# Splitting and joining DMA-turned attention probabilities at later places in an interleaved kernel

## The chip, the cores and the metric

The kernel runs on one core of a Trainium2 chip. The metric is the device time of one execution in microseconds (us), given as the median of several runs; lower is better. A profile of one execution stands beside it.

## The reference

The input is 128 graphs of 64 nodes with 768 features in float32, and a boolean adjacency per graph. Two layers follow one another, both with a residual and a layer norm:

```python
# layer 0: 12 heads of 64, additive attention, gated
h = einsum('bnd,ade->bane', x, W); th = tanh(h)
attn = leaky(th @ w_src + swap(th @ w_dst)); attn = where(adj, attn, -999); attn = softmax(attn)
feat = elu(attn @ h + b);  gate = sigmoid(x @ H_w.T + H_b)
x = layernorm(x + gate * feat + (1 - gate) * x)
# layer 1: 6 heads of 128, dot-product attention under the same adjacency
q, k, v = (heads(x @ Wi + bi) for Wi, bi in ((Wq, bq), (Wk, bk), (Wv, bv)))
probs = softmax(q @ k.T / sqrt(128) + where(adj, 0, -9e15))
x = layernorm(x + (probs @ v) @ Wf + bf)
```

The change touches layer 1's attention alone.

## The kernel before

All arithmetic is float32. The 8192 rows are 64 tiles of 128 rows (two graphs each). Every large matrix product is a block product of seven products instead of eight (a `Job`); one such product is three 128-deep slices, six matmul instructions in the profile.

**The first stage** (until about 1530 us) does layer 0 for all tiles, projects the values of layer 1, and leaves the layer's rows (`x1_d`), their transposes (`x1T_d`) and the values (`v_d`) in DRAM. The change isn't in it.

**The second stage** works on 16 groups `g` of four tiles (eight graphs). Group 0 has its queries and keys begun in the first stage. From group 1 on a group is four stretches of 14 products each: three **feature pairs** (`fc` = 0, 1, 2), each of a query job and a key job for heads `fc` and `fc + 3`, and one **output pair**, which multiplies the contexts of the group before by `Wf`. I call them the first, second and third feature pair and the output pair. The order of the 14 products in a pair is `WOVEN`: q1 k1 q2 k2 q6 k6 q5 q7 k5 k7 q4 q3 k4 k3. Products 1, 6, 7 and 4 of a job add up in one PSUM bank `y`, 5 and 3 in a bank `z`, 2 stands alone in a bank `x`. So q6 may start only when ACT has copied q1's result out of `y` (L346), q7 only after q6's copy, q4 after q7's; the same for k. The results of `x` and `z` are added by DVE (L347).

The order of instructions on each engine's queue is written by hand. `step(job, i)` issues the product and then `flush()`, the way out of the product **before** it. `woven` then resumes the side generators once each, in a fixed order:

```python
        for k, i in order:
            step(pair[k], i)
            for s in sides:
                next(s, None)
```

The sides are, in this order: `older` (the attention begun in the last pair), `done` (the last layer norm and the stores, in a first feature pair), `rows` (`residuals`, in a third feature pair: it loads the residual rows `y` (L496), has POOL add the bias to them (L503), and DVE form the block sums for the output pair (L195 to L198)), and `attend` (the attention begun now). An attention's `yield`s therefore say beside which product of which pair each of its parts is issued. It is resumed 14 times as `attend` in its own pair, then 14 times as `older` in the next. Counting these resumptions, the attention whose probabilities are turned by DMA does:

| part | engine, line | resumption before |
|---|---|---|
| scores `sp` | PE L374 | 3 |
| mask and maximum `sc`, `mx` | DVE L383, L391 | 4 |
| subtract the maximum, exponential | DVE L393, ACT L394 | 5 |
| sum, reciprocal, normalize | DVE L398, L400, L401 | 7 |
| split: copy low and high 16-bit halves apart (two copies) | ACT L416 | 8 |
| write the halves to DRAM (`halvesd`) | SP L419 | 9 |
| two transposing DMAs back into `sc` | SP L427 | 12 |
| join: weave the halves together into `scT` (two copies) | ACT L434 | 15 (step 1 of the next pair) |
| probabilities times values `cp` | PE L460 | 20 (step 6 of the next pair) |
| bias and copy to `ctxT` (four) | ACT L473 | 21 (step 7 of the next pair) |

After a pair, the next attention is created and resumed once, which puts eight loads of its values `v` (L362) on SP's queue. Then SP's queue holds what comes next in program order: the residual rows of L496 at step 1 of a third feature pair, or the four loads `a` of the next group (L307) ahead of an output pair. SP issues in order: a DMA that waits holds back those behind it.

The very last attention (group 15, `fc` = 2) turns its probabilities on PE instead. In the last output pair it is resumed twice a step, and is followed by that group's own `residuals`, whose sums read the contexts of all heads.

Of the kernel before, what the change touches and what calls it, by code (L numbers as in the profile page):

```python
# [91 lines left out]
def kernel(  # L92
# [35 lines left out]
    def bank(tag, name, bufs=2):  # L128
        return ps.tile([P, 512], F32, tag=tag, name=name, bufs=bufs)
# [47 lines left out]
    def all_of(steps):  # L177
        for s in steps:
            s()
# [80 lines left out]
    def step(job, i):  # L260
        job.product(i)
        flush()
        behind.append((job, i))
# [19 lines left out]
    def load_adj(pool, t0, n, name):  # L283
        a = pool.tile([P, n, N], U8, tag="adj", name=name, bufs=2)
        nc.sync.dma_start(
            out=a, in_=adj[t0 * P : (t0 + n) * P, :].rearrange("(t p) m -> p t m", p=P)
        )
        return a
# [64 lines left out]
    def attention(g, fc, bias, by_dma=True):  # L353

        sb = pools["late"]
        qT, kT = qk.pop((g, fc))

        v = sb.tile([P, GT, 2, E1], F32, tag="v1", name=f"v1_{g}_{fc}")
        for a in range(2):
            c0 = (a * J1 + fc) * E1  # L360
            for i in range(GT):
                nc.sync.dma_start(  # L362
                    out=v[a * N : (a + 1) * N, i, :, :],
                    in_=v_d[GT * g + i][:, c0 : c0 + E1].rearrange("(g m) e -> m g e", m=N),
                )
        yield
        yield
        yield
        sp = bank("m", f"sp_{g}_{fc}")
        for i in range(GT):  # L370
            for a in range(2):
                for gr in range(2):
                    at = slice(i * P + gr * N, i * P + (gr + 1) * N)
                    T.matmul(  # L374
                        sp[gr * N : (gr + 1) * N, (i * 2 + a) * N : (i * 2 + a + 1) * N],
                        qT[:, a, at],
                        kT[:, a, at],
                        start=True,
                        stop=True,
                    )  # L380
        yield
        sc = sb.tile([P, GT, 2, N], F32, tag="sc", name=f"sc_{g}_{fc}")
        V.tensor_tensor(  # L383
            sc,
            sp.rearrange("p (i a m) -> p i a m", i=GT, a=2),
            bias.unsqueeze(2).to_broadcast([P, GT, 2, N]),
            ALU.add,
        )
        sc3 = sc.rearrange("p i a m -> p (i a) m")
        mx = small.tile([P, 2 * GT], F32, tag="mx1", name=f"mx1_{g}_{fc}")  # L390
        V.tensor_reduce(mx, sc3, AX.X, ALU.max)  # L391
        yield
        V.tensor_tensor(sc3, sc3, mx.unsqueeze(2).to_broadcast([P, 2 * GT, N]), ALU.subtract)  # L393
        S.activation(sc, sc, AF.Exp, scale=SCALE)  # L394
        yield
        yield
        den = small.tile([P, 2 * GT], F32, tag="den1", name=f"den1_{g}_{fc}")
        V.tensor_reduce(den, sc3, AX.X, ALU.add)  # L398
        rden = small.tile([P, 2 * GT], F32, tag="rden1", name=f"rden1_{g}_{fc}")
        V.reciprocal(rden, den)  # L400
        V.tensor_tensor(sc3, sc3, rden.unsqueeze(2).to_broadcast([P, 2 * GT, N]), ALU.mult)  # L401
        scT = sb.tile([P, GT * P], F32, tag="scT", name=f"scT_{g}_{fc}")
        if by_dma:


            yield
            apart, turned = (
                t.bitcast(U16).rearrange("p (h e) -> p h e", h=2)
                for t in (scT, sc.rearrange("p i a m -> p (i a m)"))
            )  # L410
            words, wordsT = (
                t.bitcast(U16).rearrange("p (e h) -> p h e", h=2)
                for t in (sc.rearrange("p i a m -> p (i a m)"), scT)
            )
            for h in range(2):
                S.copy(apart[:, h], words[:, h])  # L416
            yield
            dr = halves_d[(g * HK + fc) % 2]
            nc.sync.dma_start(  # L419
                out=dr.rearrange("h i p c -> p h i c"),  # L420
                in_=apart.rearrange("p h (i c) -> p h i c", c=P),
            )
            yield
            yield
            yield
            for h in range(2):
                nc.sync.dma_start_transpose(  # L427
                    out=turned[:, h], in_=dr[h].rearrange("i p c -> (i p) c")
                )
            yield  # L430
            yield
            yield
            for h in range(2):
                S.copy(wordsT[:, h], turned[:, h])  # L434
            yield
            yield
            yield
            yield
            yield
        else:  # L440
            yield
            yield
            sT = bank("m", f"sT_{g}_{fc}")
            for i in range(GT):
                T.transpose(
                    sT[:, i * P : (i + 1) * P], sc[:, i].rearrange("p a m -> p (a m)"), ident
                )
            yield
            S.copy(scT, sT)
            yield  # L450
            yield
        cp = [bank("m", f"cp_{g}_{fc}_{a}") for a in range(2)]
        for i in range(GT):
            for gr in range(2):
                at = slice(i * P + gr * N, i * P + (gr + 1) * N)
                for a in range(2):
                    rows = slice(a * N, (a + 1) * N)
                    for half in range(2):
                        e = slice(half * N, (half + 1) * N)
                        T.matmul(  # L460
                            cp[a][e, at], v[rows, i, gr, e], scT[rows, at], start=True, stop=True
                        )
        yield
        if g not in ctxT:
            ctxT[g] = [
                sb.tile([P, KC, W2], F32, tag="ctxT", name=f"ctxT_{g}_{pr}", bufs=4)
                for pr in range(2)
            ]

        for a in range(2):  # L470
            hd = a * J1 + fc
            for pr in range(2):
                S.activation(  # L473
                    ctxT[g][pr][:, hd, :],
                    cp[a][:, pr * W2 : (pr + 1) * W2],
                    AF.Identity,
                    bias=bias_c["v"][:, hd : hd + 1],
                )
# [80 lines left out]
    def woven(pair, *sides, order=WOVEN):  # L559
# [5 lines that stand above are left out]
# [467 lines left out]
    with ExitStack() as ph:  # L1032
# [24 lines left out]
        attend, older, done = attention(0, 0, biases[0]), nothing, nothing  # L1057
        next(attend)
        for g in range(NG):
            last = g == NG - 1  # L1060
            rows = residuals(g - 1, False) if g > 0 else last_weight()
            for fc in range(HK):
                if (g, fc) == (0, 0):
                    continue
                if fc == 1 and not last:
                    adjs[g + 1] = load_adj(sb, GT * (g + 1), GT, f"adjg_{g + 1}")
                if fc == 2 and not last:
                    biases[g + 1] = mask_bias(g + 1)
                if (g, fc) == (0, 1):
                    pair, order = (jobs["Q"], jobs["K"]), LAST_REST  # L1070
                else:
                    query_tiles(g, fc)
                    pair, order = feature_jobs(g, fc), WOVEN
                sides = [older] + [done] * (fc == 0) + [rows] * (fc == 2)
                woven(pair, *sides, attend, order=order)
                drain(*sides)
                older, attend = attend, attention(g, fc, biases[g], not (last and fc == 2))
                next(attend)
            if not last:
                sums = load_group(g + 1, G if g else (V, G))  # L1080
                if g:
                    all_of(sums)
                else:
                    done = in_turn(sums)
            if g > 0:
                pair = out_job(2 * g - 2), out_job(2 * g - 1)
                if last:
                    attend = chain(attend, residuals(g, True))
                woven(pair, older, *[attend] * (1 + last))
                drain(older)  # L1090
                if last:
                    drain(attend)
                older, attend = attend, nothing
                done = finish(2 * g - 2, 2 * g - 1)
        p = 2 * NG - 2
        pair = out_job(p), out_job(p + 1)
# [55 lines left out]
```

## Time and profile before

| | before |
|---|---|
| median of 3 runs | 3005.59 us (3001.39 to 3006.67) |
| profiled execution, its own time | 3001.74 us |
| its span, first to last instruction | 2999.9 us |
| PE busy | 2915.2 us (97%) |
| DVE, ACT, POOL busy | 1886.1, 1095.7, 830.3 us |
| mean granted TensorE clock | 0.992 |
| second stage | about 1530 to 3000 us |

PE is TensorE, DVE VectorE, ACT ScalarE, POOL GpSimd, SP the engine that issues all DMAs here; "PEld" are PE's weight loads. A row of the timeline gives start, duration, engine, line, operation, output<-inputs, shape, and in brackets how long the engine was idle before it and who ended the wait. Neighbouring rows of PE overlap a little, since matmuls are pipelined and their ends are modelled. A row of the table of stretches gives a stretch of time, its length, each engine's busy time with the number of instructions, the granted TensorE clock, the DMA engines' share and their GB/s.

### The profile page before, as it was taken

The page shows a single profiled execution, that of the slowest core. Times are in us where ns is not written, and L with a number is a line of the kernel's source. Part 1 is how long each engine was busy: PE and PEld are TensorE (multiplying, and loading weights), DVE is VectorE, ACT ScalarE, POOL GpSimd, SP SyncE. Part 2 cuts the span into 40 slices and gives each one's busy share as a digit, 9 for nine tenths or more (in the row PEclk, how much of TensorE's full clock was granted, in tenths as well). Part 3 has the DMA queues.
Part 4 walks back from the last instruction along what each step waited for, and adds up shares of the span by engine and source line. Part 5 has one row for each costly group of instructions (what it writes and reads, how often), then busy time and mean ns, then how long its engine had stood idle before and what let it go on. Part 6 is the DMA issues. An engine that isn't in the chain of part 4 may idle for free.

```text
span 2999.9 us, 45190 instructions
## 1 busy us (share of the span) xinstructions
PE 2915.2 (97%) x17860; PEld 2007.5 (67%) x17860; DVE 1886.1 (63%) x3019; ACT 1095.7 (37%) x1902; POOL 830.3 (28%) x648
## 2 busy tenths in 40 slices
PE   7999999999999999999899999999999999999998
PEld 4566666666666666666577777777777777777775
DVE  6878878888888788788834444444344444444445
ACT  2444444444444444444433333233322332332332
POOL 2333324324333333333401212211122211122121
PEclk9999999999999999999999999999999999999999
DMA  5333333333333334333433222232222323223322
GB/s 171 127 101 117 118 111 115 106 120 112 109 120 117 104 115 128 101 117 117 153 119 80 84 78 94 84 99 74 81 94 78 103 78 97 71 89 96 98 72 78
DMA packets 279700, 309.47 MB, mean 103 GB/s; under 512 B 146753, under 2 KB 213313, under 8 KB 279489
## 3 DMA queue, kind: packets, MB, share of 16 engines
q1 hardware_dynamic: 279488, 306.58, 32.2%
q8 instruction: 142, 2.33, 0.3%
q14 instruction: 70, 0.57, 0.1%
HBM read 167.81 MB, written 113.38 MB: 94 GB/s over the span
## 4 chain that ended last, share of the span: by engine, by line
PE 88%; DVE 8%; ACT 2%; DMA 1%; SPq 1%; issue 0%; POOL 0%; POOLq 0%; DVEq 0%; ACTq 0%
PE y_o L225 8%; PE y_v L225 8%; PE y_h L225 8%; PE y_g L225 8%; PE y_q L225 7%; PE y_k L225 7%; PE z_o L225 4%; PE z_v L225 4%; PE z_h L225 4%; PE z_g L225 4%; PE z_q L225 4%; PE z_k L225 3%; PE x_k L225 2%; PE x_o L225 2%; PE x_q L225 2%; PE x_h L225 2%
## 5 line engine op out<-in xcount | busy, mean ns | idle before, releaser
L503 POOL TENSOR_TENSOR y<-y,bf_bc 128x768 f32<-128x768 f32 x64 | 130.6, 2071 | 546.0 <-DMA y<-x1d 504.1
L841 POOL TENSOR_TENSOR x<-gate,x 128x768 f32<-128x768 f32 x64 | 117.4, 1835 | 323.8 <-ACT gate L892 309.0
L527 DVE TENSOR_TENSOR y<-y_o,y 128x384 f32<-128x384 f32 x128 | 71.3, 557 | 181.5 <-PE y_o L225 156.4
L225 PE MATMUL y_q<-a,w_wq 128*128 128x256 f32 x576 | 146.1, 391 | 32.4 <-ACT qT L346 32.4
L714 POOL TENSOR_TENSOR th<-th,wsd 128x768 f32<-128x768 f32 x64 | 117.3, 1833 | 182.4 <-DVE th L713 182.4
L225 PE MATMUL y_q<-sq_q,w_wq 128*128 128x256 f32 x576 | 142.2, 383 | 10.3 <-DVE sq_q L196 8.3
L394 ACT ACTIVATE sc<-sc 128x512 f32<-128x512 f32 x48 | 30.2, 630 | 325.4 <-DVE sc L393 325.4
L225 PEld LDWEIGHTS y_q<-a,w_wq 128*128 128x128 f32 x576 | 110.3, 194 | 56.9 <-ACT qT L346 38.8
L347 DVE TENSOR_TENSOR kT<-z_k,kT 128x256 f32<-128x256 f32 x96 | 40.7, 423 | 171.3 <-PE z_k L225 99.1
L225 PE MATMUL z_q<-sq_q,w_wq 128*128 128x256 f32 x576 | 145.9, 390 | 0.0
L225 PE MATMUL y_h<-w_wq,xT 128*128 128x384 f32 x384 | 136.2, 491 | 8.6 <-DMA w_wq<-in_w_dram 7.9
L347 DVE TENSOR_TENSOR qT<-z_q,qT 128x256 f32<-128x256 f32 x96 | 40.8, 425 | 164.6 <-ACT qT L346 101.1
L225 PE MATMUL y_k<-sq_q,hw_wk 128*128 128x256 f32 x576 | 141.1, 381 | 1.4 <-ACT kT L346 1.4
L225 PE MATMUL y_k<-a,hw_wk 128*128 128x256 f32 x576 | 141.3, 382 | 0.0
L225 PE MATMUL y_h<-w_wq,sx_x 128*128 128x384 f32 x384 | 136.5, 492 | 4.2 <-ACT h L674 4.2
L225 PE MATMUL z_k<-sq_q,hw_wk 128*128 128x256 f32 x576 | 140.0, 379 | 0.0
L225 PE MATMUL y_v<-wv,sv_v 128*128 128x384 f32 x384 | 136.6, 492 | 3.0 <-DVE sv_v L196 3.0
L225 PE MATMUL z_v<-wv,sv_v 128*128 128x384 f32 x384 | 137.5, 494 | 1.7 <-DVE v L704 1.7
L225 PE MATMUL z_h<-w_wq,sx_x 128*128 128x384 f32 x384 | 137.6, 495 | 0.5 <-DVE w_wq L171 0.5
L225 PE MATMUL y_g<-hw_wk,sx_x 128*128 128x384 f32 x384 | 135.0, 488 | 2.5 <-DVE hw_wk L174 2.2
L225 PE MATMUL y_v<-wv,x1T 128*128 128x384 f32 x384 | 136.1, 491 | 1.2 <-ACT x1T L791 1.0
L713 DVE TENSOR_TENSOR th<-th,wsd 128x768 f32<-128x768 f32 x64 | 67.6, 1056 | 108.7 <-ACT th L712 108.7
(175 smaller groups left out, 6730.8 us busy)
## 6 DMA issues: line engine op xcount, KB each, us to landing
x<-in_x_dram SPq DMA_DIRECT2D x64, 384.0 KB, 3.6
dd<-dstd SPq DMA_DIRECT2D x128, 192.0 KB, 3.4
x1d<-x SPq DMA_DIRECT2D x64, 384.0 KB, 2.6
x1Td<-x1T SPq DMA_DIRECT2D x32, 768.0 KB, 4.8
vd<-v SPq DMA_DIRECT2D x64, 384.0 KB, 2.9
a<-x1Td SPq DMA_DIRECT2D x64, 384.0 KB, 4.7
v<-vd SPq DMA_DIRECT2D x384, 64.0 KB, 2.3
y<-x1d SPq DMA_DIRECT2D x64, 384.0 KB, 4.4
```

The costliest lines, as they stand in the source:

```text
L225: T.matmul(to[:, : self.n], lhsT, rhs, start=kc == 0 and not more, stop=kc == HK - 1, skip_group_check=more,)
L347: lambda mn, bk_: V.tensor_tensor(at(*mn), bk_, at(*mn), ALU.add),
L394: S.activation(sc, sc, AF.Exp, scale=SCALE)
L503: G.tensor_tensor(y, y, pools["bf"], ALU.add)
L527: V.tensor_tensor(at(*mn), b, at(*mn), ALU.add)
L713: V.tensor_tensor(th[:, 0, :], th[:, 1, :], wsd[:, 0, :], ALU.mult)
L714: G.tensor_tensor(th[:, 1, :], th[:, 1, :], wsd[:, 1, :], ALU.mult)
L841: G.tensor_tensor(xp, st[t]["gate"], xp, ALU.mult)
```

## The change

Every part from the split on moves to a later resumption; no instruction is added or removed.

| part | before | after |
|---|---|---|
| split | 8 | 9 |
| write to DRAM | 9 | 10 |
| transposes | 12 | 13 |
| join | 15 (step 1) | 19 (step 5) |
| `cp` | 20 (step 6) | 22 (step 8) |
| `ctxT` | 21 (step 7) | 23 (step 9) |

In the last output pair `older` is now resumed twice a step too, so that the join is at its step 3, `cp` at step 4 and `ctxT` at step 5.

```diff
@@ attention, by_dma @@
             yield
+            yield
             apart, turned = (
...
                 nc.sync.dma_start_transpose(
                     out=turned[:, h], in_=dr[h].rearrange("i p c -> (i p) c")
                 )
-            yield
-            yield
-            yield
+            for _ in range(6):
+                yield
             for h in range(2):
                 S.copy(wordsT[:, h], turned[:, h])
-            yield
-            yield
             yield
             yield
             yield
@@ output pair @@
-                woven(pair, older, *[attend] * (1 + last))
+                woven(pair, *[older, attend] * (1 + last))
```

## The prediction

> **What bounds the kernel.** I read the busy line first, then who PE waits for in the second stage, then a table of its stretches, then one third feature pair in the timeline.
>
> ```profile
> PE 2915.2 (97%) x17860; PEld 2007.5 (67%) x17860; DVE 1886.1 (63%) x3019; ACT 1095.7 (37%) x1902; POOL 830.3 (28%) x648
> ```
>
> PE is the bound. From group 1 on, PE waits longer than 0.1 us for one thing only. The waits of PE and of ACT between 1590 and 2940 us (total us, times, longest):
>
> ```profile
> PE y_q L225 <- ACT qT L346: 33.3, 20, 2.2
> ...
> ACT scT L434 <- DMA sc<-halvesd: 88.6, 45, 5.5
> ...
> ACT scT L416 <- DVE sc L401: 58.4, 39, 3.0
> ```
>
> The join's wait for its DMA (88.6 us) is the larger one, and looks like the target; but PE's 20 waits are for `qT`, and the stretches say where they lie. I cut the stage at the first product of each pair. First comes group 1's second feature pair (1596.78), which has what a third one has on PE, 14 products, one `sp` and one `cp`, but no residual work beside it; then two of the 15 third feature pairs; then the sum over those 15:
>
> ```profile
> 1596.78:1617.47 20.69, 20.69 (x181) 17.83 (x180) 6.31 (x13) 8.31 (x19) 0.00 (x0) 1.00 0.22 55
> ...
> 1802.37:1827.07 24.70, 22.66 (x182) 18.93 (x181) 15.01 (x20) 7.87 (x19) 8.21 (x4) 0.93 0.34 104
> ...
> 1987.85:2011.42 23.57, 21.23 (x182) 17.67 (x180) 15.58 (x20) 7.73 (x18) 8.21 (x4) 1.00 0.34 106
> ...
> sum 356.16, PE 322.84 PEld 270.34 DVE 229.56 ACT 115.47 POOL 123.05; mean PE 21.52 PEld 18.02 DVE 15.30 ACT 7.70 POOL 8.20
> ```
>
> The 20.69 us of the first are all PE. So 15 x 20.7 = 310.5 us is the floor of the third pairs, and 356.2 - 310.5 = **45.7 us** is lost in them. All other feature and output pairs are gapless: 19.42, 19.41 and 29.66 us, equal in every group. Of the 45.7, 33.3 are the waits; in 4 of the 15 pairs the clock then falls to half for 3.4 us (the 0.93 above), 4 x 1.7 = 6.8 us; the remaining 5.6 go with the gaps' edges.
>
> The cause, in the pair from 1987.85:
>
> ```profile
> 1994.30 8.21 POOL L503 TENSOR_TENSOR y<-y,bf_bc 128x768 f32<-128x768 f32 x4 [35.06 <-DMA y<-x1d]
> ...
> 1994.92 1.60 DVE L196 TENSOR_TENSOR so_o<-so_o,ctxT 128x384 f32<-128x384 f32 x1
> ...
> 1996.45 2.30 DVE L393 TENSOR_TENSOR sc<-sc,mx 128x512 f32<-128x512 f32 x1
> ...
> 1999.83 1.56 PE L225 MATMUL y_q<-sq_q,w_wq 128*128 128x256 f32 x6 [0.18 <-ACT qT L346]
> ...
> 2003.79 0.69 DVE L401 TENSOR_TENSOR sc<-sc,rden 128x512 f32<-128x512 f32 x1
> ...
> 2004.57 1.14 ACT L416 COPY scT<-sc 128x512 uint16<-128x512 uint16 x2 [2.98 <-DVE sc L401]
> 2005.62 0.47 ACT L346 ACTIVATE qT<-y_q,bq_c 128x256 f32<-128x256 f32 x1
> ...
> 2006.13 1.56 PE L225 MATMUL y_q<-a,w_wq 128*128 128x256 f32 x6 [2.16 <-ACT qT L346]
> ```
>
> DVE reaches the normalization only at 2003.79, because each two-input operation beside POOL's four adds takes about 2.2 us (L393 takes 0.68 elsewhere). ACT stands at the split from about 2001.6. Behind the split is q7's copy, whose operands have long been there, and q4 needs it: PE loses 2.16 us. So the split, not the join, stops PE.
>
> **What the Trainium skill says.** GPSIMD Engine Reference, section 8 "Key points": GpSimd shares its SBUF interfaces with VectorE and contends with VectorE instructions that have two SBUF inputs. The trace agrees: L393 at 0.68 us without POOL, 2.30 with it. TensorE: Matmul & The Clock Gate, section "Architectural detail": ACT and DVE are strict FIFO. The trace agrees: q7's copy starts as the split ends. The same page, "Part 1: The HAM clock gate": half clock after idle, judged in a free-running window of 3413 ns. The trace shows four stretches of 3.4 us at 0.5, each right after one of these waits, and none in the other 11 groups.
>
> **The change, part by part.**
>
> *Split 8 to 9.* At step 9 the way out of q7 is issued first, so q7's copy is now ahead of the split. q4 is freed. Behind the split is now k7's copy (step 11), which k4 (step 13) needs, two products later than q4.
>
> *The write and transposes go with it, and so does SP's queue.* In the second feature pair:
>
> ```profile
> 1978.63 1.14 ACT L416 COPY scT<-sc 128x512 uint16<-128x512 uint16 x2 [0.46 <-DVE sc L401]
> ...
> 1980.28 0.47 ACT L346 ACTIVATE qT<-y_q,bq_c 128x256 f32<-128x256 f32 x1 [0.52 <-PE y_q L225]
> ```
>
> The split now follows q7's copy, 1980.65 to 1981.79 instead of 1978.63 to 1979.77: 2.0 us later. SP then goes without a pause:
>
> ```profile
> 1979.79 0.40 SPq L419 DMA_DIRECT2D halvesd<-scT  x1
> 1982.43 2.44 SPq L427 DMA_TRANSPOSE sc<-halvesd  x2
> 1984.97 5.67 SPq L362 DMA_DIRECT2D v<-vd  x8
> 1990.68 2.01 SPq L496 DMA_DIRECT2D y<-x1d  x4
> ```
>
> so the residual rows come 2.0 us later and POOL's adds start at 1996.3 instead of 1994.30. Counted from the pair's start, the 15 groups have POOL's start at 5.8 to 6.8 now and 7.8 to 8.8 after. L196 (from 7.07, 0.55 us) and L393 (7.55 to 8.24) then run ahead of POOL, and the exponential, q6's and k6's copies end near 9.3 and 9.7, 2 us earlier than now (11.9 and 12.3). That matters because of the next part.
>
> *cp from step 6 to 8.* Today its 1.1 us of PE lies between k6 and q7 and hides most of ACT's delay (only 0.18 us shows). After, q7 comes at 10.34 (two products of 1.29 from 7.75). It needs q6's copy: with 9.3 there is 1 us to spare; with today's 11.9 PE would wait 1.6.
>
> *Rest of the pair.* With POOL at P = 7.8 to 8.1 (9 groups), L197, L198 and the normalization each lose one 2.05-us add: normalization ends at P + 6.35 = 14.5 at worst. `ctxT`, now behind q7's copy, runs from cp's end 12.9 to 14.5 (four, 1.57 together). Split to 15.7, k7's copy 16.2; k4 at 18.1: free. DVE's add of q7 comes behind one more blocked sum, P + 8.8 = 16.6 to 16.9; q3 at 16.8 needs it: 0 to 0.2 us, I take 0.1 for nine groups, 1 us.
>
> *Join, step 1 to 5.* Two copies of 0.76 us. In a third pair they meet ACT idle from 3.3 to 8.3, and their data lands near 0.4. In a first pair ACT is idle for 3.18 us ahead of the layer norm (2044.3 to 2047.5): 1.53 fits. In an output pair ACT has nothing else. Nothing. If that cover were gone, 1.53 us in one pair per group, 23 us. The join's 88.6 us of waiting vanishes for no gain of its own.
>
> *First pair.* `ctxT` and two norms now precede k7's copy, which ends near 2056.6; k4 is at 2057.8. Nothing, with 1.2 us to spare. *Output pair:* the write is about 3 us later; the loads `a` were issued ahead, and their POOL sums have some 16 us to spare. *Group 0 to 1:* one 8.3-us wait for `a` behind slow transposes stays; 0 to 2 us worse, I take 0.5.
>
> *Last output pair.* cp two steps earlier than the PE-turned one's frees its PSUM banks: the waits of 0.93 and 0.40 us at 2947 to 2949 go, -1.3.
>
> Sum: -45.7 + 1.0 + 0.5 - 1.3 = **-45.5 us**. On the profile's own time, 3001.74 (span 2999.9 and 1.8 around it), 2956; it lay 3.9 below the median of the runs, so from the median **2960**.
>
> **Rivals.**
>
> *The wait moves to q7 (24%).* If POOL's adds don't start later (the rows are held by something else than the queue), q7 starts at 11.98 as now, and the pair is 11.98 + 7 x 1.295 + 1.1 + 0.3 = 22.4 us. Gain 356.2 - 15 x 22.4 = 20, and with the last pair's waits time 2985. For it: q6's copy is already late in five groups. Against: SP's queue shows no pause to take up the 2 us. Delays in between give values in between.
>
> *No difference (4%).* The copies freed are used up elsewhere, 3006.
>
> *Slower (11%): the join holds ACT.* At step 5 it stands ahead of the exponential and of q6's copy in all three feature pairs and cannot be passed. In a third pair its data is due at 0.4. From its start to the end of q6's copy are 1.53 + 0.63 + 0.47 = 2.6 us, so q7 (10.34) suffers when it comes after 7.7; q7 to the pair's end is 10.5, today's mean pair 23.7, so the pair is slower than today when the data comes after about 10.6. At 11.5 it costs 0.8 x 15 = 12 us, 3018. Against: it takes 10 us of delay, and the worst write (9.2 us against 2.6) and transpose (4.3 against 2.5) together give 8.4.
>
> *That the change does not do what it says* is hard to see: the order on each queue follows from the yields.
>
> **How the numbers follow.** Main case 61%: 2954 to 2968. With the q7 case up to 2990 the range holds some 8 in 10. A measurement of this kernel tells about 0.2% (6 us). Faster: 61 + 24, 0.85; same 0.04; slower 0.11.
>
> **What would show it.** Third pairs of 20.7 to 20.9 us; no clock of 0.5 after 1600 us; PE's wait for `qT` near 0; POOL's L503 starting about 8 us into the pair and L393 back near 0.7 us; join without a DMA wait in feature pairs. Wrong if q7 waits 1 us or more in each third pair, or if first, second or output pairs are no longer 19.42, 19.41 and 29.66.

## The result and the profile after

The changed kernel takes **2956.71 us** (median of 4 runs, 2955.93 to 2957.61) against 3004.31 us before in the same comparison: a ratio of 0.9842 (95% interval 0.9825 to 0.9859), 47.6 us less. The profiled execution took 2956.7 us with a span of 2954.8 us, 45.1 us below the span before.

The page's busy line: PE's share is up by one point because the span is shorter, and its busy time fell by 10.8 us, in part since a matmul at half clock counts as busy for twice as long: before, 3.40 us from 2557.70 at half clock hold 8 matmuls, 3.40 us from 2098.40 at full clock 16, and PE counts as busy throughout both.

```profile
PE 2904.4 (98%) x17860; PEld 2004.2 (68%) x17860; DVE 1876.9 (64%) x3019; ACT 1094.6 (37%) x1902; POOL 833.6 (28%) x648
```

In the waits of PE from 1520 to 2895 us (total, times, longest) one line is left, the one-time wait between group 0 and group 1. The waits for `qT` (31.2 us in this stretch before) are gone; waits of less than 0.15 us don't show in this view:

```profile
PE y_q L225 <- DVE sq_q L196: 8.3, 1, 8.3
```

In ACT's waits from 1590 us on, the join (still L434) waits 21.8 us instead of 88.6, the split (now L417) 1.3 instead of 58.4:

```profile
ACT scT L434 <- DMA sc<-halvesd: 21.8, 28, 2.7
ACT scT L417 <- DVE sc L401: 1.3, 6, 0.2
```

The join's remaining waits all lie at the beginning of output pairs, where ACT has nothing else; in the feature pairs it never waits for its DMA.

The table of stretches, cut as before at each pair's first product: two third feature pairs and the sum over all 15.

```profile
1796.03:1817.13 21.10, 20.97 (x182) 17.75 (x180) 15.02 (x20) 8.20 (x17) 8.47 (x4) 1.00 0.39 119
...
1975.20:1995.90 20.70, 20.70 (x181) 17.83 (x180) 14.68 (x20) 8.20 (x17) 8.62 (x4) 1.00 0.42 127
...
sum 312.85, PE 312.08 PEld 267.00 DVE 223.65 ACT 122.96 POOL 126.10; mean PE 20.81 PEld 17.80 DVE 14.91 ACT 8.20 POOL 8.41
```

The third pairs went from 356.16 to 312.85 us. Nine of them are at the floor of 20.70, six take 21.1. All first, second and output pairs between are still 19.42, 19.41 and 29.66 us. No stretch of half clock lies between 1600 us and the last 5 us. So 43.3 of the 45.1 us come from the third pairs; the last output pair and its tail (from 2932.44 to 2999.9 before, 2888.93 to 2954.8 after) give 1.6, and all that lies ahead of the first third pair 0.2.

The timeline of the pair from 1975.20, with the rows that answer to those shown of before:

```profile
1982.28 0.55 DVE L196 TENSOR_TENSOR so_o<-so_o,ctxT 128x384 f32<-128x384 f32 x1
1982.74 0.69 DVE L393 TENSOR_TENSOR sc<-sc,mx 128x512 f32<-128x512 f32 x1
...
1983.83 8.62 POOL L501 TENSOR_TENSOR y<-y,bf_bc 128x768 f32<-128x768 f32 x4 [37.23 <-DMA y<-x1d]
...
1987.04 0.47 ACT L346 ACTIVATE qT<-y_q,bq_c 128x256 f32<-128x256 f32 x1 [2.12 <-PE y_q L225]
1988.13 1.57 ACT L471 ACTIVATE ctxT<-cp,bv_c 128x256 f32<-128x256 f32 x4 [0.61 <-PE cp L458]
...
1989.58 1.15 ACT L417 COPY scT<-sc 128x512 uint16<-128x512 uint16 x2
...
1990.92 0.47 ACT L346 ACTIVATE kT<-y_k,bk_c 128x256 f32<-128x256 f32 x1 [0.20 <-PE y_k L225]
```

POOL's adds begin 8.63 us into the pair instead of 6.45. L196 and the subtraction L393 are through by then, at 0.55 and 0.69 us. q7's copy stands ahead of the split and starts as soon as its product is there, and k7's copy behind the split waits for nothing but PE.

### The profile page after: what moved, and what is told of

Read it like the earlier page. It is cut to its first block, busy times and chain, and to the rows that moved or that the text cites. A ratio compares the mean times of both kernels' runs of the same rounds, so it can differ in the third digit from the quotient of the medians.

```text
span 2954.8 us, 45191 instructions
## 1 busy us (share of the span) xinstructions
PE 2904.4 (98%) x17860; PEld 2004.2 (68%) x17860; DVE 1876.9 (64%) x3019; ACT 1094.6 (37%) x1902; POOL 833.6 (28%) x648
## 4 chain that ended last, share of the span: by engine, by line
PE 91%; DVE 5%; DMA 1%; ACT 1%; SPq 1%; issue 0%; POOL 0%; POOLq 0%; DVEq 0%; ACTq 0%
PE y_o L225 8%; PE y_v L225 8%; PE y_h L225 8%; PE y_k L225 8%; PE y_g L225 8%; PE y_q L225 7%; PE z_o L225 4%; PE z_v L225 4%; PE z_h L225 4%; PE z_k L225 4%; PE z_q L225 4%; PE z_g L225 4%; PE x_k L225 2%; PE x_o L225 2%; PE x_q L225 2%; PE x_h L225 2%
## 5 line engine op out<-in xcount | busy, mean ns | idle before, releaser
L346 ACT ACTIVATE qT<-y_q,bq_c 128x256 f32<-128x256 f32 x144 | 67.3, 468 | 308.4 <-PE y_q L225 308.4
L225 PE MATMUL y_q<-a,w_wq 128*128 128x256 f32 x576 | 140.1, 379 | 1.0 <-ACT qT L346 1.0
L277 POOL TENSOR_TENSOR rs_a<-ve_a,minus_half 128x1 f32<-128x1 f32 x64 | 36.0, 563 | 359.2 <-DVE ve_a L275 359.2
L225 PE MATMUL z_g<-hw_wk,sx_x 128*128 128x384 f32 x384 | 134.4, 486 | 0.0
```

The lines of the kernel that those rows point to most:

```text
L225: T.matmul(to[:, : self.n], lhsT, rhs, start=kc == 0 and not more, stop=kc == HK - 1, skip_group_check=more,)
L277: G.tensor_tensor(rstd, ve, minus_half, ALU.pow)
L346: lambda mn, bk_: S.activation(at(*mn), bk_, AF.Identity, bias=bias(mn[1])),
```

## The experiments

None of the eight kernels leaves out any part of the reference. The question was which of the moved parts brings the time: the change moves the split past q7's copy, delays SP's queue and with it the residual rows, moves `cp`, and moves the join that gives the change its name. "Rows" below are the residual rows (L496) that POOL's four adds wait for. Medians of before differ between the comparisons (3005.32 us in the first four, 3001.55 in the last four), so ratios are given.

**The split without the join.** Split, write and transposes one resumption later; the join stays three products behind, `cp` and `ctxT` where they were.

```diff
             yield
+            yield
             apart, turned = (
...
                 S.copy(wordsT[:, h], turned[:, h])
             yield
-            yield
             yield
             yield
             yield
```

> Of the kernel before, only the split, the write and the transposes move one resumption later (9, 10, 13); the join goes to 16, so that it is still three products behind the transposes, and the products cp (20), ctxT (21) and the last output pair stay as they were. Theory (the split stood in front of q7's copy, and its delay also delays the residual rows on SP's queue): the third feature pairs fall from 23.7 to 20.7-21.1 us, only the 1.6 us of the last output pair are missing: 2958 us. Rival (the time came from the join's distance to its DMA): the join still waits, at most a few us are gained, 2995-3004 us.

Measured: 2959.62 us, ratio 0.985 (0.9836 to 0.9865). Eight third pairs at 20.70 us and seven at 21.1; in the last output pair the two waits of 0.93 and 0.40 us for PSUM banks are still there. The join's distance is not needed for the gain.

**The join without the split.** Join 19, `cp` 22, `ctxT` 23 and the doubled resumption at the end; the split where it was.

```diff
             for h in range(2):
                 nc.sync.dma_start_transpose(...)
-            yield
-            yield
-            yield
+            for _ in range(7):
+                yield
             for h in range(2):
                 S.copy(wordsT[:, h], turned[:, h])
-            yield
-            yield
             yield
             yield
             yield
...
-                woven(pair, older, *[attend] * (1 + last))
+                woven(pair, *[older, attend] * (1 + last))
```

> Of the kernel before, only the join (19), cp (22), ctxT (23) and the doubled resumption in the last output pair are taken over; the split, the write and the transposes stay at 8, 9, 12. Theory: the third feature pairs keep some 23.6 us: q7 now waits about 1.6 us because cp no longer lies ahead of it, q4 waits the rest, and the copy of q7 still ends about 18.2 us into the pair; only fewer stretches of half clock and the last output pair may give something: 2996-3003 us. Rival (the join's distance does it): 2965 us or less.

Measured: 2992.13 us, ratio 0.996 (0.9945 to 0.9975), somewhat more gain than expected. PE's waits from 1590 us on, and the pair from 1800.03 in the timeline:

```profile
PE y_q L225 <- ACT qT L346: 28.9, 29, 1.8
```

```profile
1811.36 1.56 PE L225 MATMUL y_q<-sq_q,w_wq 128*128 128x256 f32 x6 [0.82 <-ACT qT L346]
...
1816.10 1.14 ACT L416 COPY scT<-sc 128x512 uint16<-128x512 uint16 x2 [4.43 <-DVE sc L401]
1817.14 0.47 ACT L346 ACTIVATE qT<-y_q,bq_c 128x256 f32<-128x256 f32 x1
...
1817.66 1.56 PE L225 MATMUL y_q<-a,w_wq 128*128 128x256 f32 x6 [0.86 <-ACT qT L346]
```

The wait is not removed, it is divided: part of it is now at q7, because `cp` no longer lies ahead of it, and the rest at q4 behind the split. The third pairs sum to 347.1 us, 9.0 less than before. None of the shorter waits was followed by half clock, which is worth 4 x 1.7 = 6.8 us of it.

**The rows late, nothing else.** The order of attention is that of before; three loads that nobody reads are put on SP's queue ahead of the rows.

```diff
                 next(attend)
+                if g > 0 and fc == 1:
+                    for a, i in ((0, 0), (1, 0), (0, 1)):
+                        nc.sync.dma_start(out=spare[a * N : (a + 1) * N, i], in_=v_d[i]...)
```

> The kernel before with its order of attention untouched; three loads of values into a spare tile that nobody reads are put on SP's queue between the values and the residual rows of a third feature pair, so that the rows, and POOL's adds, come about 2 us later. Theory: POOL's adds start 8-9 us into the pair, the subtraction takes 0.7 us again, the normalization ends at 11.4-14.6; the split stays in front of q7's copy, so where the normalization is late (6 to 9 pairs) q4 still waits about 0.8 us: third pairs 20.7 to 22, 2963-2970 us. Rival (the order of split and copy is what counts, the rows' lateness is a by-product): third pairs stay above 22.5 us, 2990-3004 us.

Measured: 2961.23 us, ratio 0.9857 (0.9842 to 0.9871). POOL's adds begin 7.7 to 9.7 us into the pair, with the subtraction through. Nine third pairs are at 20.70, six at 21.55, and PE waits

```profile
PE y_q L225 <- ACT qT L346: 3.6, 6, 0.6
```

In the pair from 1975.77, the subtraction starts ahead of POOL's adds, and the split in front of q7's copy costs PE nothing:

```profile
1983.30 0.69 DVE L393 TENSOR_TENSOR sc<-sc,mx 128x512 f32<-128x512 f32 x1
...
1984.44 8.57 POOL L503 TENSOR_TENSOR y<-y,bf_bc 128x768 f32<-128x768 f32 x4 [37.28 <-DMA y<-x1d]
...
1987.55 1.15 ACT L416 COPY scT<-sc 128x512 uint16<-128x512 uint16 x2
...
1988.90 0.47 ACT L346 ACTIVATE qT<-y_q,bq_c 128x256 f32<-128x256 f32 x1 [0.20 <-PE y_q L225]
```

So delaying the rows by 2 us, with the split still in front of q7's copy, gives nearly the whole gain. That the split stands in the way matters only while DVE is late.

**The rows early, in the changed kernel.** The rows' loads are issued after the fifth load of values instead of after the eighth.

```diff
-def attention(g, fc, bias, by_dma=True):
+def attention(g, fc, bias, by_dma=True, between=None):
...
                 nc.sync.dma_start(out=v[...], in_=v_d[...])
+                if between and (a, i) == (1, 0):
+                    between()
...
         if last:
             sums = sum_tiles(early, "sq", W2, f"o{g}")
+        else:
+            yield
...
-                older, attend = attend, attention(g, fc, biases[g], not (last and fc == 2))
+                older, attend = attend, attention(
+                    g, fc, biases[g], not (last and fc == 2),
+                    (lambda: next(rows)) if g > 0 and fc == 1 else None,
+                )
```

> The changed kernel, but in a third feature pair the loads of the residual rows are issued after the fifth of the eight loads of values instead of after the eighth, so that POOL's adds start 2 us earlier, about where they did in the kernel before (6 to 7 us into the pair). Theory: the subtraction meets POOL's adds again, q6's copy ends at about 11.9 and q7, with cp no longer ahead of it, waits 1.6 us; q4 does not wait: third pairs 22.4 us, 2980 us, up to 7 more where the clock is halved. Rival (moving the split is all that counts): unchanged, 2957 us.

Measured: 2977.24 us, ratio 0.9912 (0.9896 to 0.9929). POOL's adds begin 5.9 to 6.8 us into the pair; third pairs 21.9 to 22.8. The subtraction (L395 in this kernel) is slow again, and now it is q7 that waits, in all 15 pairs; q4 does not:

```profile
1986.45 8.20 POOL L505 TENSOR_TENSOR y<-y,bf_bc 128x768 f32<-128x768 f32 x4 [34.78 <-DMA y<-x1d]
...
1988.60 2.29 DVE L395 TENSOR_TENSOR sc<-sc,mx 128x512 f32<-128x512 f32 x1
...
1990.92 0.63 ACT L396 ACTIVATE sc<-sc 128x512 f32<-128x512 f32 x1 [6.11 <-DVE sc L395]
...
1991.97 1.56 PE L225 MATMUL y_q<-sq_q,w_wq 128*128 128x256 f32 x6 [1.19 <-ACT qT L346]
```

This is the first rival of the prediction made real, and near the numbers that it was given: third pairs of 22.2 us on average against 22.4, 2977 us against 2985.

**The split later, rows early, cp not moved.** The first and the fourth edit together.

> As split_only (split 9, write 10, transposes 13, join 16, cp and ctxT where they were in the kernel before), with the residual rows issued after the fifth load of values as in rows_early, so that POOL's adds start where they did in the kernel before. It is the order of split and copy alone: neither the rows' delay nor the move of cp. Theory: cp lies ahead of q7 again and hides all but 0 to 0.6 us of its wait; q4 is free; q3 waits 0 to 0.9 us for DVE's add of q7, which comes behind the late normalization: third pairs 21.2 to 22, 2963-2972 us, some 10 below rows_early (2977). Rival (cp's place is indifferent): as rows_early, 2975-2980 us.

Measured: 2964.72 us, ratio 0.9876 (0.9861 to 0.9891). POOL's adds begin 5.8 to 7.2 us into the pair. Third pairs take 20.8 to 22.1 us; q7 waits in four of them (0.10 to 0.76 us), of which the view of PE's waits from 1590 us on shows three:

```profile
PE y_q L225 <- ACT qT L346: 1.7, 3, 0.8
```

Against the kernel before it gains 37 us by the order of split and copy alone; against the rows-early kernel above, which differs in the join, `cp` and `ctxT`, it is better by 0.0036 of the time, 11 us. With DVE late, `cp` ahead of q7 is cover, and the change takes it away. No run moves `cp` alone, so this is read from the traces: in the rows-early kernel the join ends 4.6 us into the pair and ACT then idles for 6.11 us, as the line of L396 above shows, so it isn't the join that q7 waits for; and `ctxT` comes behind q7's copy.

Put together, with the ratio to before. Where the split is later, "rows as before" means that the earlier issue puts them back; with the order of before, "2 us later" means the three unread loads:

| | rows as before | rows 2 us later |
|---|---|---|
| order as before | 1 | 0.9857 |
| join, `cp`, `ctxT` later | 0.996 | not tried |
| split later | 0.9876 | 0.985 |
| split, join, `cp`, `ctxT` later | 0.9912 | 0.9842 (the change) |

Either the later split or the later rows alone would give at least three quarters of the gain, and together they give little more than the rows alone. They are two cures of one fault, DVE's lateness beside POOL's adds. The later split of the *second* pair brings the later rows of the third one along.

**q3's remaining wait.** The second half of the residual side one step later.

```diff
         for pr in range(PAIR):
+            if pr and not last:
+                yield
             for y in ys[2 * g + pr]:
```

> The changed kernel, with the second half of the residual side (two of POOL's adds and the block sums of the second pair of tiles) issued one step later, so that DVE's add of q7 stands ahead of the first of those sums instead of behind it. Theory (q3's waits of 0.11 to 0.14 us in six third pairs are for that add): they vanish, all 15 third pairs 20.70 us, 2.4 us in all: 2954 us, not to be told from the changed kernel's 2957 by the runs, but in the trace. Rival (the add is late for another reason): six pairs stay at 21.1.

Measured: 2955.17 us, ratio 0.9844 (0.9829 to 0.9858), not to be told from the change by the runs. In the trace all 15 third pairs are 20.70 us, the sum over them with PE busy throughout; the wait was for DVE's add behind a blocked sum:

```profile
sum 310.47, PE 310.47 PEld 267.48 DVE 213.83 ACT 122.87 POOL 125.66; mean PE 20.70 PEld 17.83 DVE 14.26 ACT 8.19 POOL 8.38
```

**The wait between group 0 and 1.** The last load of group 1's rows `a` is issued at step 13 of group 0's third pair, ahead of the transposes.

```diff
+        def last_block():
+            for _ in range(12):
+                yield
+            load_x1T(1, 1, 1)
...
                 sides = [older] + [done] * (fc == 0) + [rows] * (fc == 2)
+                if (g, fc) == (0, 2):
+                    sides.append(last_block())
```

> The changed kernel, with the last of the four loads of group 1's rows (a) issued at step 13 of group 0's third pair, ahead of the transposes and the eight loads of values, instead of behind them. Theory: PE's 8.3-us wait near 1580 us is for this load behind the queue; it becomes 0 to 1 us, and the 10 us of half clock after it go too (5 us): 2943-2945 us. Rival (the load is late because the DMA engines are full then): the wait stays above 5 us, 2953-2957 us.

Measured: 2947.02 us, ratio 0.9815 (0.9798 to 0.9832). SP's part of the timeline shows the load (L307) 8.4 us earlier than the 1574.24 of the changed kernel:

```profile
1565.80 0.32 SPq L307 DMA_DIRECT2D a<-x1Td  x1
1568.56 2.44 SPq L428 DMA_TRANSPOSE sc<-halvesd  x2
1571.06 5.15 SPq L362 DMA_DIRECT2D v<-vd  x8
```

PE's wait of 8.3 us and the 10 us of half clock are gone. The first pair of group 1, 31.8 us in the changed kernel (1564.82 to 1596.58), takes 20.7: 11.1 us, not the 13 expected, since about half of the half clock lay within the wait. This profiled execution came 2.1 us later to that pair than the changed kernel's, by waits and half clock of the first stage, where nothing was edited; counted from the pair's start, the load is 10.5 us earlier.

**Both together.**

> The changed kernel with both the early load of early_block and the later second half of later_half. Theory: the two add up, 2941 us. Rival: 2953 or more.

Measured: **2942.87 us** (2940.81 to 2944.5), ratio 0.9802 (0.9788 to 0.9817), the fastest of all, 2 us from the sum expected. From 1520 to 2880 us its PE has no wait over 0.1 us.

## Why the prediction was right, step by step

- **The place and size of the loss.** 45.7 us in the third pairs, of which 44.7 were forecast to come back: 43.3 did. That the whole sum (-45.5) comes within 0.4 us of the profile's (45.1 in span) is in part luck: these 1.4 us less are made up by 0.7 us more ahead of the third pairs and 0.3 in the last output pair.
- **The split moves behind q7's copy; k7's copy behind it is in time.** Right: k7's copy waits for PE, not for ACT. As the cause, though, the step claims too much. "So the split, not the join, stops PE" is right about the join, but the kernel with late rows keeps the split where it was and loses only 3.6 us of waits to it. The cause is DVE's lateness; the split is where it was felt.
- **SP's queue carries the 2.0 us to the rows and to POOL.** Right: the write of the second pair, POOL's start (forecast 7.8 to 8.8, measured 7.8 to 10.0) and the subtraction's 0.7 us are as worked out. One ground for the last was missing: with POOL at 7.8 to 8.1 in nine groups and the subtraction ending at 8.24, the prediction's own numbers have POOL begin before it ends. In seven groups POOL did (7.78 to 8.21), and the subtraction still took 0.68 to 0.69 us, since it had begun first; POOL's first add was the one delayed (see the end). The later end of the range comes from the loads' landing (the first one 5.5 us after issue in the latest group, 3.3 in the earliest) and does no harm.
- **cp's move uncovers q7 by 1.6 us unless DVE is early.** Right: with early rows q7 waited 0.96 to 1.83 us.
- **q3's wait, 1 us in all.** Undersized: six pairs of 21.1 us, 2.35 us in all. The term took 0.1 us in nine groups. Measured were six groups, those with POOL's start at or before 8.0, with 0.11 to 0.14 us of waiting and some 0.27 us more at the gap's edges, which this term had left out, though the sum over the third pairs had counted them. DVE's add ended at 17.05 (pair from 1796.03), not at 16.6 to 16.9: the normalization ended at 14.6, and POOL's four adds took 8.3 to 8.5 us instead of 8.2, which the forecast did not allow for, so that the sum behind them came free later.
- **The join costs nothing at step 5.** Right in all three feature pairs. In the third pair it runs at 3.16, behind k1's copy.
- **Group 0 to 1, +0.5.** Measured +0.1 (8.35 us of wait against 8.26).
- **Last output pair, -1.3.** Measured -1.6: both waits for banks are gone.
- **Profile to median.** The sum gave 2956 on the profile's own time, measured 2956.7. The forecast of 2960 added the 3.9 us that the profile of before lay below its median; the changed kernel's profile lies at its median, so the whole term was too much, and the forecast came out 3.3 us high.

Of the rivals, the wait at q7 is a real mechanism, held off by the late rows alone. The join that holds ACT did not come about; data arriving 10 us late was not tried.

## What to carry to other kernels

When an engine's queue is written out by hand, find for each wait of the bounding engine the instruction that stands *in front* of the one it waits for, and then what makes that one late: here the larger wait, for a DMA at the join (88.6 us), cost nothing, and the smaller one at the split (58.4 us) stood where 45.7 us of PE's time were lost. Follow a moved instruction through the DMA queue as well: a write that is issued 2 us later delayed loads of another part of the kernel, and such a delay alone, without the move, gives most of the gain. Work placed ahead of a waiting product is cover, and should be moved only when the product's operand is early.

## What the runs showed of the hardware

- The delay between DVE and POOL goes both ways, and in these pairs the operation that began first kept its time. A subtraction of 0.68 us took 2.30 when it came to POOL's running adds. POOL's four adds, 8.21 us in the pair from 1987.85 before, took 8.62 in the pair from 1975.20 after. The difference is in the first add alone, 2.21 us instead of 1.81, as it came while L198 was running; the other three took 2.13 to 2.26 us, against 2.12 to 2.27 before, though L401 (1.35 us instead of 0.69) fell among them. Other third pairs after bear this out: the first add took 2.11 us where 0.44 us of the subtraction were left as it began (pair from 2778.67), 1.90 where 0.22 were left (1885.62), and 1.81 where DVE was at L398, a reduction with one input (2242.76).
- The subtraction shows the other side: L393 began 7.54 us into the pair and took 0.68 us with POOL's start at 7.78 (after, pair from 2778.67), but 2.30 us with POOL's start at 7.22 (split later and rows early, pair from 2157.20).
- SP issued in the order of its queue. In the changed kernel it issued the write at 1789.99, the two transposes that wait for its data at 1792.63, and the eight loads and the residual rows right behind them, at 1795.16 and 1800.36; the load that was put ahead of the transposes at 1565.80 did not wait for them.
- In the third pairs of all the kernels run, single waits of PE up to 1.83 us were never followed by half clock; of the 15 waits of 1.94 to 2.16 us before, four were, for 3.413 us each, beginning 0.1 to 0.6 us after the wait's end. Which four is a matter of phase: the half clock began at 1636.12, 1820.44, 2557.72 and 2834.20 us, whole multiples of 3.413 us apart (54, 216 and 81). Cut at this grid, the four waits have 1.94 to 2.15 us within one step; of the other eleven, ten have at most 1.78 in any step, and one has 1.94 and was not followed. So the 6.8 us that half clock costs before are in part chance. In the 8.3-us wait the half clock began about 3 us into the wait and lasted 10.24 us, three times 3.413. The Trainium skill, TensorE: Matmul & The Clock Gate, "Part 1: The HAM clock gate", gives a window of 3413 ns that runs free, which agrees with these lengths, with the grid, and with only some of equal waits being hit. That half clock comes after at least one idle window of about 3.4 us, as the same section has it, does not agree: waits of 1.94 to 2.15 us were enough here.
